# An attention and feed-forward block in fp32: one sum of the query rotation, two NF4 steps and four weight splits moved at the start of the attention loop

## The chip, the cores and the metric

The kernel runs on one core of a Trainium2 chip. The metric is the device time of one execution in microseconds. A core has TensorE (PE in the profile, its weight loads are PEld), VectorE (DVE), ScalarE (ACT), GpSimd (POOL) and SyncE (SP), which here only issues DMAs. Each engine works through its own list of instructions in order and waits on semaphores of the others.

## The reference

x has 8 sequences of 128 tokens with 512 features; ctx_4096 is the context of the same shape. Two blocks follow each other:

```
x = x + attention(layernorm(x), ctx_4096, ctx_4096, mask, Wq, Wk, Wv, Wo)
x = x + ffn(layernorm(x), w1, w2, w3)
```

The attention has 32 query heads and 8 key/value heads of 128 features, so four query heads share one key head. Queries and keys are rotated (RoPE), the logits are capped by 30 tanh(logits / 30), masked, put through a softmax, multiplied with the values and projected by Wo:

```
q = apply_rope((query @ Wq).reshape(b, t, h, d))
logits = MAX_ATTN_VAL * jnp.tanh(logits * ATTN_MULT / MAX_ATTN_VAL)
attn = einsum(softmax(where(mask, logits, -1e30)), v) @ Wo
```

The ffn first quantises its three weights (1376 x 512 or 512 x 1376) to the 16 levels of NF4, in blocks of 64 with a scale each, and turns them back to floats; then h = silu(x @ w1.T) * (x @ w2.T), and the output is h @ w3.T. All is fp32.

## The kernel before, in words

**Arithmetic.** A large product in near-fp32 is made of three fast matmuls: each operand is split into a high part (a rounded copy) and a low part (the rest), and the three products low x high, high x high and high x low are summed in PSUM (product(), L166 to L172). split() (L154) makes the two parts: a copy on ScalarE (L155) and a subtraction on an engine that the caller names, DVE or POOL (L156). One product of 512 columns over 512 contracted features is twelve matmuls.

**Stages.** The program has four stages: (1) keys, values, the layer norm of x and the first query tiles, up to 118 us; (2) the attention loop of 64 steps, from 118 to about 600 us; (3) gate and up products of the feed-forward, to 723.8 us; (4) the down product and the stores, to the end.

**The attention loop** (L762). A unit u is one key/value head and one half of the batch (four sequences); step i treats unit i // 4, sequence i % 4. The loop is a software pipeline. In step i, the order of emission is: one query tile of the next unit (q_proj, L474: twelve matmuls into one of the two banks of tag "q", then rope()); project(i - 3), the product with Wo (twelve matmuls); turn(i - 2), four transposes into a bank of tag "q" and their split; values(i - 1), the product of weights and values (matmuls into the bank "pv", on DVE a reciprocal L693 and a normalisation L694); scores(i), the logits (L678), tanh and exp on ScalarE (L681, L682), and the mask on POOL (L684). Steps 0 to 2 are special: unit 1 has its query tiles 0 and 1 in step 0, tile 2 in step 1 and tile 3 in step 2, and step 3 has none.

**rope()** (L455) rotates a query tile: two half copies on ScalarE (L463, L464), the cosine product on DVE (L465), the sine product on POOL (L466), and a closing sum (L467). For unit 1 the cosine product is written in place into the PSUM bank, and the sum runs on DVE; so the bank of tag "q" is free only when that sum is done. rope() returns the sum as a function, and the loop calls it later, through the list `later`.

**Weights.** load_o() (L657) issues the DMA of one 128 x 512 tile of Wo into a staging buffer and puts its split into `todo`; load_q() does the same for Wq. `due` (L755) says at the end of which step a split is emitted.

**NF4.** quantize() (L376) is a generator that walks over 17 pieces of the ffn weights (11 Up, 6 Down). Each piece has 15 steps, one per decision bound: an activation on ScalarE (L196) and an accumulation on DVE (L200, L202), of 128 x 1024 elements; the last piece has 96 x 512. A product with the block scales on DVE ends a piece (L280 or L238). Along the way the pieces after it are loaded (SP's DMAs) and normalised (POOL, L206). pump(n) (L405) draws steps from the generator until n credits are used up; a 128 x 1024 step costs one credit and a 96 x 512 step a half. store() (L411) emits the splits of a finished piece, one per call, and hands on what is fresh for the next call. pump() is called with 1 at the ends of steps 0 and 1, with 1.5 and 1.65 in steps 3 to 57, with 1 and 2 in step 58, with 3.45 or 2.6 for each gate/up product, and with 2 for each of the first twelve entries of the down list:

```
        if (b, i) in most:
            if i == 1:
                product(pd[b], mine, stop=False)
                mine.clear()
            pump(2)
            store()
```

The down stage takes w3 in eleven tiles w3t_0 to w3t_10. The first twelve entries use w3t_0 to w3t_7, those behind them w3t_8 to w3t_10. split_h() (L841) splits one part of h per entry, on ScalarE and DVE, four entries ahead.

Of the kernel before, what the change touches and what calls it, by code (L numbers as in the profile page):

```python
# [23 lines left out]
G = NH // NKV  # L24
# [38 lines left out]
def block_kernel(ctx: ExitStack, tc: tile.TileContext, x, ctxt, mask, wq, wk, wv, wo, w1, w2, w3, w12t, w3_t,  # L63
                 rope_tab, nf_bias, out):
    nc = tc.nc
    V, S, Q, E = nc.vector, nc.scalar, nc.gpsimd, nc.tensor
# [9 lines left out]
    def bank(tag, name):  # L76
        shape = [P, 1024 if tag == "pv" else 512]
        return ps.tile(shape, F32, tag=tag, name=name, bufs=2 if tag == "q" else 1)[:, :512]
# [75 lines left out]
    def split(hi, lo, src, engine):  # L154
        S.copy(hi, src)  # L155
        engine.tensor_tensor(lo, src, hi, ALU.subtract)  # L156
# [54 lines left out]
    class Down(Unit):  # L211
# [30 lines left out]
        def store(self, h):  # L242
            pool, tag, bufs = (f1, "w3t", 8) if h < 8 else (nf, "nf_t", 2) if h < 10 else (xp, "wide", 2)
            t = w3t[h] = pool.tile([P, 2, KT, P], F32R, tag=tag, name=f"w3t_{h}", bufs=bufs)
            own = t.rearrange("p i k c -> p i (k c)")[:self.p].rearrange("p i (c e) -> p i e c", e=4)
            split(own[:, 0], own[:, 1], self.part(self.w, h).rearrange("p (e c) -> p e c", e=4), Q)
# [44 lines left out]
    class Scales:  # L291
# [23 lines left out]
        def turn(self, tag):  # L315
            pt = bank(tag, f"pt_ar_{self.h}")[:2 * 16, :P]
            E.transpose(pt, self.s.rearrange("p t b -> p (t b)"), ident)

            def later():
                t = nf.tile([2 * 16, P], F32, tag="nf_st", name=f"art_{self.h}", bufs=1)  # L320
                S.copy(t, pt)
                nc.sync.dma_start(scale_d.rearrange("t j b h -> (t j b) h")[:, self.h * P:(self.h + 1) * P], t)
            stored.append(later)
# [81 lines left out]
    def pump(n):  # L405

        credit[0] += n
        while credit[0] > 0:
            credit[0] -= next(stream, n + credit[0])
# [7 lines left out]
    def end_store():  # L417
        if stored:
            stored.pop()()
# [7 lines left out]
    with ExitStack() as c1:  # L427
# [11 lines left out]
        def stage(src, shape, name):  # L439
            if early:  # L440
                raw = early.pop(0)
            else:
                raw = raw_pool[-1].tile([P, 512], F32, tag="raw", name=f"raw_{name}", bufs=3 if len(raw_pool) > 1 else 4)
            if len(shape) == 3:
                raw = raw.rearrange("p (k n) -> p k n", k=shape[1])
            nc.sync.dma_start(raw, src)
            return raw
# [21 lines left out]
        wqt, todo = {}, {}  # L469

        def load_q(kv, g):
            wqt[kv, g], todo["q", kv, g] = columns(wq, kv * G + g, f"wq_{kv}_{g}")

        def q_proj(u, g):  # L474
            kv, half = divmod(u, 2)
            if g == 0:
                qr[u] = a1.tile([P, 4, G, T], F32, tag="qr", name=f"qr_{u}", bufs=2)
            pq = bank("q", f"pq_{u}_{g}")
            w, t = wqt[kv, g], xT[half]
            product(pq, [((w[:, 0, k], w[:, 1, k]), (t[:, 0, k], t[:, 1, k])) for k in range(KT)])  # L480
            return lambda: rope(qr[u][:, :, g, :], pq, cosq, sgnq, f"q{u}_{g}", V if u < 2 else None, u == 1)
# [175 lines left out]
        def load_o(kv, g):  # L657
            h = kv * G + g
            raw = stage(wo[h * HD:(h + 1) * HD], [P, D], f"wo_{kv}_{g}")
            t = wot[kv, g] = at.tile([P, 2, D], F32R, tag="wo", name=f"wo_{kv}_{g}", bufs=8)  # L660
            todo["o", kv, g] = lambda: split(t[:, 0], t[:, 1], raw, Q if kv else V)

        def load_kv(kv):
            for half in range(2):
                krt[kv, half] = at.tile([P, 512], F32, tag="kr", name=f"krt_{kv}_{half}", bufs=4)
                nc.sync.dma_start(krt[kv, half], kr_d[kv, half])
            vt[kv] = at.tile([P, B, HD + 1], F32, tag="v", name=f"vt_{kv}")
            nc.sync.dma_start(vt[kv][:, :, :HD], v_d[kv])
            Q.memset(vt[kv][:, :, HD:], 1.0)

        def where(i):
            u, bb = divmod(i, 4)
            return u, u // 2, (u % 2) * 4 + bb, bb

        def scores(i):
            u, kv, b, bb = where(i)
            pl = bank("s", f"pl_{i}")
            E.matmul(pl, krt[kv, u % 2][:, bb * T:(bb + 1) * T], qr[u][:, bb].rearrange("p g t -> p (g t)"),  # L678
                     start=True, stop=True)
            th = at.tile([P, 512], F32, tag="th", name=f"th_{i}", bufs=3)  # L680
            S.activation(th, pl, AF.Tanh, scale=ATTN_MULT / CAP)  # L681
            S.activation(th, th, AF.Exp, scale=CAP)  # L682
            em[i] = th.rearrange("p (g t) -> p g t", g=G)
            Q.tensor_tensor(em[i], em[i], mt.unsqueeze(1).to_broadcast([P, G, T]), ALU.mult)  # L684

        def values(i):
            u, kv, b, bb = where(i)
            ad[i] = at.tile([P, G, HD], F32, tag="ad", name=f"ad_{i}")
            pv = ps.tile([P, G, 256], F32, tag="pv", name=f"pv_{i}", bufs=1)
            for g in range(G):  # L690
                E.matmul(pv[:, g, :HD + 1], em[i][:, g], vt[kv][:, b], start=True, stop=True)  # L691
            rs = tp.tile([P, G], F32, tag="rs", name=f"rs_{i}")
            V.reciprocal(rs.unsqueeze(2), pv[:, :, HD:HD + 1])  # L693
            V.tensor_tensor(ad[i], pv[:, :, :HD], rs.unsqueeze(2).to_broadcast([P, G, HD]), ALU.mult)  # L694
# [5 lines left out]
        def project(i):  # L700
            u, kv, b, bb = where(i)
            po = bank("wo", f"po_{i}")
            product(po, [((aT[i][:, 0, g], aT[i][:, 1, g]), (wot[kv, g][:, 0], wot[kv, g][:, 1]))
                         for g in range(G)])
            V.tensor_tensor(acc[b], acc[b], po, ALU.add)
# [19 lines left out]
        def load_w12(h):  # L725
            w12[h] = [wp.tile([P, 2, KT, P], F32R, tag="wq", name=f"w12_{h}_{j}", bufs=6) for j in range(2)]
            for j in range(2):
                nc.gpsimd.dma_start(w12[h][j], w12t_d[h, j])
# [23 lines left out]
                V.tensor_tensor(hT[half, h // 4][:, h % 4], sg, pu, ALU.mult)  # L752
            return later

        due = {0: [("o", 0, 0), ("o", 0, 1)], 1: [("o", 0, 2), ("o", 0, 3)]}  # L755
        xn = {}

        def turned(ks, tags):
            for f in [normal2(k, xn[k], tag) for k, tag in zip(ks, tags)]:
                f()  # L760

        for i in range(N):  # L762
            u, kv, b, bb = where(i)
            s8 = i % 8
            if kv + 1 < NKV:
                if s8 == 0:
                    load_kv(kv + 1)
                if s8 < 4:
                    load_q(kv + 1, s8)
                else:  # L770
                    load_o(kv + 1, s8 - 4)
                due.setdefault(i + (2 if i < 4 else 1), []).append(("q" if s8 < 4 else "o", kv + 1, s8 % 4))
            tiles = {0: (0, 1), 1: (2,), 2: (3,), 3: ()}.get(i, (bb,)) if u + 1 < 2 * NKV else ()
            later = [q_proj(u + 1, g) for g in tiles]
            later = [f() for f in later[:1]] + later[1:]
            if i == 0:
                later.pop(0)()
            if i > 3:
                store()
                end_store()  # L780
            pump(1.5 if 2 < i < 58 else 1 if i == 58 else 0)
            if 0 <= i - 3:
                project(i - 3)
            if i in (59, 61):
                ln = LayerNorm((i - 59, i - 58), f"y{i - 59}")
            if 0 <= i - 2:
                turn(i - 2)
            if 59 <= i < 63:
                ln.sums(i - 59)
            if 0 <= i - 1:  # L790
                values(i - 1)
            scores(i)
            if i == 0:
                later = [later[0]()]
            if i == 61:
                xn.update({k: pair.rows(k, "xn") for k in (0, 1)})
            for f in later:
                f()
            pump(1.65 if 2 < i < 58 else 2 if i == 58 else 1 if i < 2 else 0)
            if i == 62:  # L800
                turned((0, 1), "qq")
            if i in (60, 62):
                ln.finish(Q)
                pair = ln
            for k in due.pop(i, ()):
                todo[k]()
            if i >= 61:
                load_w12(i - 61)
# [63 lines left out]
    for b, i in down:  # L872
# [5 lines left out]
        for h in range(4 * i, min(NHT, 4 * i + 4)):  # L878
            m = min(P, H - h * P)
            t, s = w3t[h].rearrange("p i k c -> p i (k c)"), hs[b, i]  # L880
# [7 lines left out]
        elif i == 2:  # L888
            o = f1.tile([P, D], F32, tag="o", name=f"o_{b}", bufs=4)
# [41 lines left out]
```

## Time and profile before

| | us |
|---|---|
| median of 3 runs | 789.2 |
| lowest, highest | 789.14, 790.14 |
| the profiled execution | 790.01 |
| its span, first to last instruction | 788.2 |
| PE busy | 778.0 |
| DVE busy | 627.9 |
| ACT busy | 586.4 |
| POOL busy | 466.4 |

The span is what the instructions cover; 1.8 us of the execution lie around it. Groups of instructions are named by line, engine, operation and tiles (out<-in); a bracket at a line's end tells how long the engine was idle before it and who released it. Matmuls are pipelined: the twelve of one product take about 2.72 us from the first start to the start of what follows, while each shows 0.4 us of its own. The mean granted clock of TensorE over the span is 0.998 of full speed.

### The profile page before, as it was taken

How to read it: one execution, taken by the hardware profiler on the slowest of the kernel's cores; microseconds unless marked ns; L12 is line 12 of the kernel's file. 1: busy time of each engine (PE TensorE's matmuls, PEld its weight loads, DVE VectorE, ACT ScalarE, POOL GpSimd, SP SyncE). 2: the span in 40 equal slices, each digit the busy share in tenths (PEclk: the TensorE clock that was granted, in tenths of full speed). 3: DMA queues.
4: the chain of work that ended last, by engine and by line, in shares of the span. 5: the costliest groups of instructions: out<-in, count | busy, mean ns of one | idle time of the engine just before them, and what ended most of it. 6: DMA issues, size and time to landing. Idle time of an engine off the chain costs nothing. (4 is left out here: it accounts for less than half of the span.)

```text
span 788.2 us, 11198 instructions
## 1 busy us (share of the span) xinstructions
PE 778.0 (99%) x3737; PEld 627.3 (80%) x3737; DVE 627.9 (80%) x840; ACT 586.4 (74%) x821; POOL 466.4 (59%) x411
## 2 busy tenths in 40 slices
PE   8999998999999999999999999999999999999998
PEld 6788886778777878778787877888778888888877
DVE  5767777888888887888888878879878688888981
ACT  7358667989796978879797979898732678778840
POOL 3568544688787878777797877878652223232100
PEclk9999999999999999999999999999999999999999
DMA  7966735355437344526337432414133235652011
GB/s 228 300 195 195 214 105 154 108 143 176 89 121 206 135 107 121 174 55 218 103 100 203 131 94 94 125 65 134 43 119 107 57 108 157 186 162 53 5 54 54
DMA packets 73329, 102.44 MB, mean 130 GB/s; under 512 B 7832, under 2 KB 42840, under 8 KB 73272
## 3 DMA queue, kind: packets, MB, share of 16 engines
q1 hardware_dynamic: 70104, 90.19, 38.2%
q0 software_dynamic: 3168, 11.54, 4.7%
q8 instruction: 30, 0.49, 0.3%
q14 instruction: 27, 0.22, 0.1%
HBM read 79.32 MB, written 22.38 MB: 129 GB/s over the span
## 5 line engine op out<-in xcount | busy, mean ns | idle before, releaser
L202 DVE SCALAR_TENSOR_TENSOR nc_w<-nm_w,nc_w 128x1024 f32<-128x1024 bf16 (+1 forms) x238 | 284.6, 1196 | 60.2 <-ACT nm_w L196 49.8
L196 ACT ACTIVATE nm_w<-w_w,bias 128x1024 bf16<-128x1024 f32 (+1 forms) x255 | 276.2, 1115 | 14.9 <-DVE nc_w L202 7.9
L172 PE MATMUL pq<-xT,wq 128*128 128x512 f32 x768 | 209.3, 422 | 0.0
L172 PE MATMUL po<-wo,aT 128*128 128x512 f32 x768 | 190.1, 396 | 0.0
L172 PEld LDWEIGHTS pq<-xT,wq 128*128 128x128 f32 x768 | 143.9, 188 | 55.9 <-issue 24.4
L172 PEld LDWEIGHTS po<-wo,aT 128*128 128x128 f32 x768 | 143.8, 189 | 34.5 <-issue 2.9
L684 POOL TENSOR_TENSOR th<-th,mt 128x512 f32<-128x512 f32 x64 | 83.8, 1310 | 87.9 <-ACT th L682 80.0
L466 POOL TENSOR_TENSOR rs_q<-rs_q,sgnq 128x512 f32<-128x512 f32 x64 | 82.9, 1295 | 14.7 <-ACT rs_q L464 14.7
L681 ACT ACTIVATE th<-pl 128x512 f32<-128x512 f32 x64 | 38.3, 598 | 53.5 <-PE pl L678 51.3
L467 POOL TENSOR_TENSOR qr<-rc_q,rs_q 128x512 f32<-128x512 f32 x56 | 72.5, 1295 | 0.0
L691 PE MATMUL pv<-vt,th 128*128 128x129 f32 x512 | 67.9, 276 | 0.1
L678 PE MATMUL pl<-qr,krt 128*128 128x512 f32 x128 | 66.4, 601 | 0.0
L172 PE MATMUL pg<-xT,w 128*128 128x512 f32 x264 | 63.7, 390 | 0.0
L172 PE MATMUL pu<-xT,w 128*128 128x512 f32 x264 | 63.5, 389 | 0.0
L691 PEld LDWEIGHTS pv<-vt,th 128*128 128x128 f32 x512 | 62.2, 192 | 0.7 <-POOL th L684 0.7
L172 PE MATMUL pd<-w3t,hs 128*128 128x512 f32 (+3 forms) x297 | 60.8, 366 | 0.4 <-POOL w3t L156 0.4
L172 PEld LDWEIGHTS pd<-w3t,hs 128*128 128x128 f32 (+1 forms) x297 | 51.3, 189 | 9.9 <-POOL w3t L156 0.8
L206 POOL TENSOR_TENSOR w_w<-w_w,s_w 128x1024 f32<-128x1024 f32 (+1 forms) x17 | 39.6, 2329 | 33.0 <-DMA s_w<-scale_d 31.6
L172 PEld LDWEIGHTS pu<-xT,w 128*128 128x128 f32 x264 | 49.6, 188 | 10.3
L172 PEld LDWEIGHTS pg<-xT,w 128*128 128x128 f32 x264 | 49.3, 188 | 10.1
L156 POOL TENSOR_TENSOR w3t<-w_w,w3t 128x512 fp32r<-128x512 f32 (+1 forms) x11 | 17.2, 1564 | 65.7 <-ACT w3t L155 65.7
L155 ACT CAST aT<-pt_a 128x512 fp32r<-128x512 f32 x64 | 36.6, 571 | 24.9 <-PE pt_a L162 24.9
(119 smaller groups left out, 1103.7 us busy)
## 6 DMA issues: line engine op xcount, KB each, us to landing
w12t_d<-dqt SPq DMA_DIRECT2D x22, 512.0 KB
w<-w12t_d POOLq DMA_DIRECT2D x22, 512.0 KB, 4.6
s_w<-scale_d SPq DMA_DIRECT2D x40, 256.0 KB
raw_wq<-in_L_xattn_Wq SPq DMA_DIRECT2D x32, 256.0 KB
raw_wo<-in_L_xattn_Wo SPq DMA_DIRECT2D x32, 256.0 KB
s_w<-scale_d SPq DMA_DIRECT2D x86, 64.0 KB
ws<-in_L_ffn_w SPq DMA_DIRECT2D x20, 256.0 KB
w_w<-in_w12t SPq DMA_DIRECT2D x10, 512.0 KB
```

Source lines behind the costliest of these rows:

```text
L155: S.copy(hi, src)
L156: engine.tensor_tensor(lo, src, hi, ALU.subtract)
L172: E.matmul(out, a, b, start=start and i + j == 0, stop=stop and i == n - 1 and j == 2)
L196: S.activation(m, self.w, AF.Relu, bias=bias[:self.p, i:i + 1], scale=BIG if up else -BIG)
L202: V.scalar_tensor_tensor(self.c, m, step, self.c, ALU.min, ALU.subtract if i == POS[0] else ALU.add)
L206: Q.tensor_tensor(self.w, self.w, self.s, ALU.mult)
L466: Q.tensor_tensor(s, s, every(sgn), ALU.mult)
L467: return lambda: (engine or Q).tensor_tensor(dst, c, s, ALU.add)
L678: E.matmul(pl, krt[kv, u % 2][:, bb * T:(bb + 1) * T], qr[u][:, bb].rearrange("p g t -> p (g t)"), start=True, stop=True)
L681: S.activation(th, pl, AF.Tanh, scale=ATTN_MULT / CAP)
L684: Q.tensor_tensor(em[i], em[i], mt.unsqueeze(1).to_broadcast([P, G, T]), ALU.mult)
L691: E.matmul(pv[:, g, :HD + 1], em[i][:, g], vt[kv][:, b], start=True, stop=True)
```

## The change

Four edits. The closing sum of a query tile in steps 1 and 2 (tiles 2 and 3 of unit 1) is emitted behind values(i - 1) and ahead of scores(i), instead of behind scores(i). The pumps at the ends of steps 0 and 1 are gone, so that the NF4 stream begins its work in the loop at step 3. The four splits of the first projection weights wo_0 to wo_3, which were emitted two at the end of step 0 and two at the end of step 1, all stand in step 1: two ahead of scores(1) and two at its end. And the subtractions of wo_2 and wo_3 run on POOL instead of DVE.

```
-            todo["o", kv, g] = lambda: split(t[:, 0], t[:, 1], raw, Q if kv else V)
+            todo["o", kv, g] = lambda: split(t[:, 0], t[:, 1], raw, Q if kv or g > 1 else V)
...
-        due = {0: [("o", 0, 0), ("o", 0, 1)], 1: [("o", 0, 2), ("o", 0, 3)]}
+        due = {1: [("o", 0, g) for g in range(G)]}
...
             if 0 <= i - 1:
                 values(i - 1)
+            if i in (1, 2):
+
+                later.pop(0)()
+                if i == 1:
+                    for _ in range(2):
+                        todo[due[1].pop(0)]()
             scores(i)
...
             for f in later:
                 f()
-            pump(1.65 if 2 < i < 58 else 2 if i == 58 else 1 if i < 2 else 0)
+            pump(1.65 if 2 < i < 58 else 2 if i == 58 else 0)
```

## The prediction

> **What bounds the kernel now.** First the page's busy shares, then the stage table, then the timelines of the two places where TensorE stops.
>
> ```profile
> PE 778.0 (99%) x3737; PEld 627.3 (80%) x3737; DVE 627.9 (80%) x840; ACT 586.4 (74%) x821; POOL 466.4 (59%) x411
> ```
>
> ```profile
> 118.00:136.10 18.10, 15.62 (x64) 10.49 (x63) 13.55 (x19) 14.22 (x22) 9.14 (x7) 0.91 0.56 169
> ...
> 200.00:300.00 100.00, 100.00 (x499) 80.09 (x497) 84.12 (x112) 83.70 (x119) 78.05 (x65) 1.00 0.43 123
> ...
> 723.80:758.40 34.60, 34.22 (x152) 28.01 (x150) 31.64 (x39) 27.86 (x40) 5.96 (x4) 1.00 0.06 14
> 758.40:788.00 29.60, 26.63 (x147) 23.14 (x147) 10.24 (x18) 2.59 (x5) 0.00 (x0) 1.00 0.19 71
> ```
>
> Columns are PE, PEld, DVE, ACT, POOL busy, granted clock, DMA share, GB/s. PE is full from 200 to 300 us with a fifth of the other engines free: there only PE's own work counts. The first row, attention steps 0 to 2, is the weak one (15.62 of 18.10 us, clock 0.91). In the third DVE works 31.64 of 34.60 us: it is full there. PE's timeline in the weak place:
>
> ```profile
> 123.91 3.00 PE L172 MATMUL pq<-xT,wq 128*128 128x512 f32 x12
> 129.36 0.63 PE L162 MATMUL pt_a<-ident,ad 128*128 128x128 f32 x4 [2.44 <-DVE qr L467]
> ...
> 131.60 4.69 PE L172 MATMUL po<-wo,aT 128*128 128x512 f32 x12
> 136.13 0.60 PE L162 MATMUL pt_a<-ident,ad 128*128 128x128 f32 x4
> ```
>
> The first attention transposes wait 2.44 us for a bank that DVE frees with the sum of the third query tile. DVE's timeline shows why that sum is late:
>
> ```profile
> 123.68 1.22 DVE L202 SCALAR_TENSOR_TENSOR nc_w<-nm_w,nc_w 128x1024 f32<-128x1024 bf16 x1
> 124.81 2.39 DVE L156 TENSOR_TENSOR wo<-raw_wo,wo 128x512 fp32r<-128x512 f32 x2
> 127.12 0.69 DVE L465 TENSOR_TENSOR pq<-pq,cosq 128x512 f32<-128x512 f32 x1
> ...
> 128.53 0.68 DVE L467 TENSOR_TENSOR qr<-pq,rs_q 128x512 f32<-128x512 f32 x1
> ```
>
> One NF4 step and two weight subtractions lie ahead of it. After the gap the granted clock is halved:
>
> ```profile
> 131.00:132.00 1.00, 1.00 (x3) 0.35 (x2) 1.00 (x2) 0.00 (x0) 0.00 (x0) 0.50 0.35 77
> ...
> 133.00:134.00 1.00, 1.00 (x4) 0.56 (x3) 0.97 (x3) 0.97 (x3) 0.04 (x1) 0.50 0.91 330
> ```
>
> With 0.87 before and 0.92 behind these rows, it is at half for some 3.4 us. The second place is the end of the NF4 stream (timelines of DVE and PE):
>
> ```profile
> 724.09 0.69 DVE L752 TENSOR_TENSOR hT<-sg,pu 128x512 f32<-128x512 f32 x1 [0.35 <-PE pu L172]
> ...
> 754.38 0.55 DVE L156 TENSOR_TENSOR hs<-hT,hs 128x384 fp32r<-128x384 f32 x1
> 754.85 0.68 DVE L238 TENSOR_TENSOR w_w<-nc_w,s_w 96x512 f32<-96x512 f32 x1
> ```
>
> ```profile
> 758.35 26.67 PE L172 MATMUL pd<-w3t,hs 96*128 96x512 f32 x147 [0.38 <-POOL w3t L156]
> ```
>
> At 724.09 DVE waits for PE, so it starts the last stage in step with it. From there it never pauses until the last NF4 product (L238) at 755.53; ScalarE's copy and POOL's subtraction bring the last weight tile w3t_10 at 758.30, and PE has already waited 0.38 us for it. The stream has no slack there.
>
> **Part 1, the sum between values and scores (steps 1 and 2).** scores() puts nothing on DVE, so DVE's order stays: multiply, reciprocal, normalise, sum. Nothing else passes it on another engine. Price 0.
>
> **Part 2, the start.** Off DVE ahead of the third tile go one NF4 step (1.22) and two subtractions (2.39), and from behind it another NF4 step; wo_0 and wo_1 now follow the sum, and wo_2 and wo_3 are POOL's, between the masks of steps 1 and 2. On ScalarE two NF4 activations (1.15, 1.13) go, and the copies of wo_0 and wo_1 (1.12) now stand after the third tile's half copies and ahead of step 1's tanh. SP moves one pair of scale loads behind three query-weight loads; it waits there for staging buffers, freed by 130 us, and the scales are used only at the unit's end, after 140 us. The chain from the old rows, as an estimate:
> - ScalarE: third tile's half copies end 123.2 (PE's sums end 121.89), wo_0 and wo_1 copies 124.3, tanh and exp 125.6, wo_2 and wo_3 copies 126.7, the fourth tile's half copies 128.2, aT copy 128.8.
> - DVE: multiply 124.4, normalise 125.2, sum 125.9; then the two wo subtractions to 127.8, multiply 128.9, aT subtraction 129.5.
> - POOL, 1.29 each: mask 1 to 126.9, wo_2 128.2, wo_3 129.5, fourth tile's sine 130.8, mask 2 132.1.
> - PE: fourth query tile unchanged at 123.91, its twelve matmuls at the pitch of 0.227 end 126.65. The bank is free since 125.9: transposes 126.65, values 127.1, scores 128.0, projection from 128.8, held by aT until 129.6, next transposes 132.0 instead of 136.13.
>
> The gain is 4.1 us. Ends: only the idle gap, 2.4; no bubble at all, 4.95 (126.65 plus 0.43, 0.90, 0.46 and 2.74 from the rows of the next step gives 131.2). I stay near the upper end because the halved clock goes with the gap. What is late next is aT, then mask 2 on POOL, with 0.3 us to spare against the values at 132.35.
>
> **Part 3, the two NF4 steps come back.** The stream is one fixed list, advanced by credits. Two credits fewer at steps 0 and 1 leave it two items behind everywhere until the last stage, whose twelve pumps of 2 had room to spare. In attention and gate/up nothing is paid: each pump issues as many items as before, PE is full there, and the moved scale and weight loads stay a whole unit ahead of use. POOL's normalise (2.40) of the second down unit now stands behind two more w12 loads that wait for PE until 631.8; it ends near 634.8, about when ScalarE first needs it. w3t_7 moves into the last stage, ready near 727.1 against its use at 728.6.
>
> In the last stage two 128x1024 steps more lie ahead of the last product. The pitch of such pairs is 2.46 (728.36 to 730.82). Since store() runs once per iteration, w3t_10 also slips one iteration, past one more hs subtraction (0.47, from 750.92 to 751.39). That is 2.93. POOL's w3t_7 and the last normalise now fall into DVE's full stretch; a subtraction beside POOL took 1.63 instead of 0.69 at 746.39. Bounds 2.4 (the steps alone) to 3.9 (one such clash); I take 3.2, nearer to the counted items. PE's wait becomes some 3.5 us instead of 0.38.
>
> Then the clock. A 2.44 us gap was followed by 3.4 us at half clock, at most 1.7 us of dense matmuls. The new gap is longer, but part of the slow time may fall into the gap itself. Bounds 0 and 1.7; I take 1.1.
>
> The Trainium skill, "TensorE: Matmul & The Clock Gate", section "Why this matters for your kernels", speaks against this change: it asks for no PE gaps over about 3 us, since an idle window returns the clock to half. By it the old gap would have been safe and the new one would not: the full 1.7 at the end and a sum of 790.8 instead of 790.2. The rows above show the drop already behind 2.44 us, and the measurement decides.
>
> **Sum.** The profiled execution took 790.01 (span 788.2 and 1.8 around it): 790.01 - 4.1 + 3.2 + 1.1 = 790.2. It stands 0.8 above the median of 789.2. If the runs at the median lack the early half clock, their gain is 3.3 and they end at the same 789.2 - 3.3 + 3.2 + 1.1 = 790.2; if they also escape the late one, at 789.1. I say 789.8, nearer to the first.
>
> **Rivals.**
> - A, above: gain at the start, given back at the end. 789.8, own range 788.6 to 791.0. Chance 0.52.
> - B, faster: the end stays covered, because DVE makes up the two steps. For it: DVE is idle for 12% of 662 to 723.8 us (54.43 busy of 61.80). Against: it waits for PE at 724.09 with the stream still two items behind. 790.01 - 4.1 = 785.9; decides if w3t_10 slips less than about 1.5 us. Chance 0.15.
> - C, slower: POOL becomes the bound at the start. If its five operations take 1.71 (mask 1 at 126.61, beside DVE's wo subtractions) instead of 1.29, mask 2 ends 2.1 later and values 2 wait 1.8: 790.2 + 1.8 = 792.0. It decides from about 0.9 us of waiting. Against: only some 2 us of DVE's subtractions overlap. Chance 0.20.
> - D, no half clock at either end in most runs: 789.2 - 3.3 + 3.2 = 789.1. Chance 0.13.
>
> The Trainium skill, "GPSIMD Engine Reference", section "Specifications", says that POOL shares its SBUF ports with VectorE when that reads two SBUF inputs. By it every subtraction of wo beside POOL is slow, which gives C; the old rows give both 1.29 and 1.71.
>
> **How the numbers follow.** 0.2% is 1.58 us, about what a measurement of this kernel can tell. A lies within it but for 0.06 above and 0.02 below; D all but 0.02 below; B is faster but for 0.02, C slower but for 0.01. Faster 0.17, same 0.58, slower 0.25. The range takes in most of B and C: 786.6 to 792.0.
>
> **What would show it.** Right: the transposes behind the fourth query tile start without a gap, the clock stays at 1.00 near 130 us, and the next come some 4 us earlier; at the end the 96-row matmul waits 3 to 4 us for POOL's w3t, with clock rows of 0.50 behind. Wrong: that wait stays under 1 us, PE waits for mask 2 near 132 us, or new PE waits appear between 140 and 720 us.

## The result, and the profile after

The changed kernel takes 794.6 us (median of six runs, 793.38 to 798.08) where the kernel before, run beside it, takes 789.55 (789.14 to 790.14). The ratio is 1.0069, 95% interval 1.0050 to 1.0088: it is slower. The prediction said 789.8 us within 786.6 to 792.0, so the measurement lies outside its range.

The profiled execution is the lowest of the six, 793.38 us with a span of 791.3. PE's timeline at the start, with start, duration, engine, line, operation and tiles, and in brackets the idle time ahead and who ended it:

```profile
126.72 0.60 PE L162 MATMUL pt_a<-ident,ad 128*128 128x128 f32 x4
...
130.25 2.56 PE L172 MATMUL po<-wo,aT 128*128 128x512 f32 x10 [0.71 <-DVE aT L156]
132.66 0.60 PE L162 MATMUL pt_a<-ident,ad 128*128 128x128 f32 x4
```

The gap of 2.44 us ahead of the first transposes is gone, and the next ones come at 132.66 instead of 136.13: the start gains 3.4 us. DVE's timeline shows what is late next:

```profile
125.06 0.68 DVE L467 TENSOR_TENSOR qr<-pq,rs_q 128x512 f32<-128x512 f32 x1
125.65 3.35 DVE L156 TENSOR_TENSOR wo<-raw_wo,wo 128x512 fp32r<-128x512 f32 x2
128.92 0.68 DVE L465 TENSOR_TENSOR pq<-pq,cosq 128x512 f32<-128x512 f32 x1
129.52 0.68 DVE L156 TENSOR_TENSOR aT<-pt_a,aT 128x512 fp32r<-128x512 f32 x1
```

The two wo subtractions take 3.35 us. POOL is busy beside them: with the mask of step 1 (L684) from 125.47 to 126.77, then with its own two.

```profile
126.74 3.40 POOL L156 TENSOR_TENSOR wo<-raw_wo,wo 128x512 fp32r<-128x512 f32 x2
```

That holds the fourth tile's multiply to 128.92 and aT to 129.52 (its duration brings it to 130.2, where the projection starts).

Then the surprise, in the attention loop. POOL's timeline and PE's at step 52:

```profile
508.44 2.41 POOL L206 TENSOR_TENSOR w_w<-w_w,s_w 128x1024 f32<-128x1024 f32 x1 [4.33 <-DMA s_w<-scale_d]
510.82 1.26 POOL L684 TENSOR_TENSOR th<-th,mt 128x512 f32<-128x512 f32 x1
```

```profile
512.13 1.16 PE L691 MATMUL pv<-vt,th 128*128 128x129 f32 x8 [0.91 <-POOL th L684]
```

Before, POOL began this L206 at 504.53 without a wait, and the mask followed in time:

```profile
504.53 2.41 POOL L206 TENSOR_TENSOR w_w<-w_w,s_w 128x1024 f32<-128x1024 f32 x1
...
509.68 1.30 POOL L684 TENSOR_TENSOR th<-th,mt 128x512 f32<-128x512 f32 x1 [0.27 <-DVE ad L694]
```

Now L206 waits 4.33 us for the scales of the eleventh and last Up piece, and the mask of step 51, queued behind it on POOL, makes the values in step 52 wait on PE. SP's issues around that place, before and after, tell why the scales are late:

```profile
497.60 0.93 SPq L275 DMA_DIRECT2D w_w<-in_w12t  x2
498.59 2.56 SPq L265 DMA_DIRECT2D s_w<-scale_d  x4
...
501.90 6.85 SPq L361 DMA_DIRECT2D scale_d<-art  x8
```

```profile
495.22 6.89 SPq L361 DMA_DIRECT2D scale_d<-art  x8
502.23 0.97 SPq L275 DMA_DIRECT2D w_w<-in_w12t  x2
503.25 2.61 SPq L265 DMA_DIRECT2D s_w<-scale_d  x4
```

The eight scale stores (L361) are emitted by the loop's end_store(), in the same step before and after; the loads (L275, L265) come from the NF4 stream. With the stream two items late the loads fall behind the stores, and the stores wait 4.2 us for ScalarE's copy (L355), as the waits of SP's queue in the profile after show:

```profile
SPq L361 <- ACT art L355: 4.2, 1, 4.2
```

The end, PE's timeline:

```profile
722.27 34.16 PE L172 MATMUL pd<-w3t,hs 128*128 128x512 f32 x150
759.69 28.43 PE L172 MATMUL pd<-w3t,hs 96*128 96x512 f32 x147 [3.26 <-POOL w3t L156]
```

The wait for the last weight tile is 3.26 us instead of 0.38, and the 147 matmuls behind it take 28.43 instead of 26.67. The stage table (columns PE, PEld, DVE, ACT, POOL busy, granted clock, DMA share, GB/s) has the reason:

```profile
760.00:761.00 1.00, 1.00 (x5) 0.78 (x4) 0.34 (x2) 0.30 (x1) 0.00 (x0) 0.79 0.00 0
761.00:762.00 1.00, 1.00 (x4) 0.81 (x3) 1.00 (x3) 0.74 (x2) 0.00 (x0) 0.50 0.00 0
762.00:763.00 1.00, 1.00 (x3) 0.72 (x3) 0.46 (x1) 0.00 (x0) 0.00 (x0) 0.50 0.69 260
763.00:764.00 1.00, 1.00 (x4) 0.81 (x3) 0.00 (x0) 0.00 (x0) 0.00 (x0) 0.51 0.01 2
764.00:765.00 1.00, 1.00 (x6) 0.82 (x5) 0.65 (x2) 0.66 (x2) 0.00 (x0) 1.00 0.00 0
```

Half clock from 760.6 to 764.0, 3.4 us.

This execution is a lucky one. A second profile of the same kernel (a2_after below) took 794.37 us, near the median, and the account is made with it beside the first. Each row is a difference of two places in PE's timeline against the same places before (first scores 118.12, next transposes 136.13, and the down product as below):

```profile
723.82 34.16 PE L172 MATMUL pd<-w3t,hs 128*128 128x512 f32 x150
```

| | predicted | first profile, 793.38 | a2_after, 794.37 |
|---|---|---|---|
| stage 1, to the first scores (L678) | 0 | -0.04 | -0.72 |
| first scores to the next transposes | -4.1 | -3.43 | -3.44 |
| from there to the down product | 0 | +1.92 | +2.44 |
| wait for the last w3t | +3.2 | +2.88 | +3.91 |
| the 147 matmuls, slower by the clock | +1.1 | +1.76 | +2.17 |
| sum | +0.2 | +3.1 | +4.4 |

The sums answer to the spans (791.3 and 792.6 against 788.2). Stage 1 differs by up to 1.0 us between executions of kernels that are alike there, so it is left out of the comparisons of the start below.

### The profile page after: what moved, and what is told of

Read it like the earlier page. It is cut to its first block, busy times and chain, and to the rows that moved or that the text cites. A ratio compares the mean times of both kernels' runs of the same rounds, so it can differ in the third digit from the quotient of the medians.

```text
span 791.3 us, 11202 instructions
## 1 busy us (share of the span) xinstructions
PE 779.4 (98%) x3737; PEld 628.3 (79%) x3737; DVE 624.7 (79%) x838; ACT 586.1 (74%) x821; POOL 470.0 (59%) x413
## 5 line engine op out<-in xcount | busy, mean ns | idle before, releaser
L684 POOL TENSOR_TENSOR th<-th,mt 128x512 f32<-128x512 f32 x64 | 83.5, 1305 | 82.6 <-ACT th L682 70.3
L172 PE MATMUL pd<-w3t,hs 128*128 128x512 f32 (+3 forms) x297 | 62.6, 373 | 3.3 <-POOL w3t L156 3.3
L678 PE MATMUL pl<-qr,krt 128*128 128x512 f32 x128 | 65.7, 595 | 0.1
L206 POOL TENSOR_TENSOR w_w<-w_w,s_w 128x1024 f32<-128x1024 f32 (+1 forms) x17 | 40.1, 2361 | 36.8 <-DMA s_w<-scale_d 34.6
```

What stands on the lines that cost most here:

```text
L172: E.matmul(out, a, b, start=start and i + j == 0, stop=stop and i == n - 1 and j == 2)
L206: Q.tensor_tensor(self.w, self.w, self.s, ALU.mult)
```

## The experiments

The theory after this reading: the start's gain is real; the two items that the stream owes cost some 2 us in the loop and 5 to 6 us at the end, and none of that has to do with the sum or the weights. The first four kernels take the change apart.

**e1_repaid: the stream's debt is paid at once.** The changed kernel, with half a credit more in steps 4 to 7.

```
-            pump(1.65 if 2 < i < 58 else 2 if i == 58 else 0)
+            pump(2.15 if 3 < i < 8 else 1.65 if 2 < i < 58 else 2 if i == 58 else 0)
```

> The changed kernel, with the two NF4 steps repaid in steps 4 to 7 (half a credit more at each of their last pumps), so that the stream is where it was before from step 8 on. Theory (the start gains about 3.5 us, and all that is lost comes from the stream being two steps late): the gain stays, the wait of TensorE near 512 us and the long wait for the last w3t are gone, and the time is 786.0 (785.3 to 787.0) against 789.5 before. Rival (the start's gain is lost again in any case, at the next place where the pipeline is tight): 789 to 790.

Measured: 786.65 us (785.83 to 787.12), ratio 0.9962 [0.9948, 0.9976]. The start keeps its gain (first scores to next transposes 14.58 us, as after; before 18.01), nothing is lost in the loop, and the end is that of before:

```profile
754.18 26.66 PE L172 MATMUL pd<-w3t,hs 96*128 96x512 f32 x147 [0.38 <-POOL w3t L156]
```

So all of the loss is the debt's. This version beats both kernels: it is 3.1 us faster than the one before.

**e2_stream: the debt alone.** The kernel before, without its pumps in steps 0 and 1.

```
-            pump(1.65 if 2 < i < 58 else 2 if i == 58 else 1 if i < 2 else 0)
+            pump(1.65 if 2 < i < 58 else 2 if i == 58 else 0)
```

> The kernel before, with only the two pumps at the ends of steps 0 and 1 taken away; the sum, the weight splits and their engines stay. Theory: it gains about 1.2 us at the start (one NF4 step of 1.22 us off DVE ahead of the third tile's multiply, the two subtractions of 2.39 us stay) and pays all of the late stream: 1.9 us in the attention loop, 2.9 at the last w3t and up to 1.8 of half clock, so 793 to 796. Rival (the loss comes from the weight splits on POOL, not from the stream): 788 to 789.5.

Measured: 796.31 us (795.68 to 796.84), ratio 1.0084 [1.0070, 1.0097]. The debt alone makes the kernel slower, as expected, by a little more than the 793 to 796 us allowed, and the sizes inside differ: the start gained 2.1 us rather than 1.2, the loop lost 1.5, and the end lost more.

```profile
761.33 29.33 PE L172 MATMUL pd<-w3t,hs 96*128 96x512 f32 x147 [4.30 <-POOL w3t L156]
```

The clock stays at half for 6.8 us here, from 760.2 to 767.0, twice as long as in the first profile after.

**e3_weights: the sum and the weight splits alone.** The changed kernel, with the two pumps put back (the reverse of e2's edit).

> The changed kernel with the two pumps at the ends of steps 0 and 1 put back: only the sum and the weight splits are moved. Theory: the third tile's sum is one NF4 step (1.2 us) later than in the changed kernel, so that 2.3 to 3.0 us of the start's gain are left, and nothing is lost later: 786.5 to 787.5. Rival (the splits on POOL cost the time): 791 or more.

Measured: 788.76 us (787.83 to 789.95), ratio 0.9989 [0.9980, 0.9998]. It gains 1.0 us and misses the expected 786.5 to 787.5. DVE's and PE's timelines:

```profile
129.74 1.22 DVE L202 SCALAR_TENSOR_TENSOR nc_w<-nm_w,nc_w 128x1024 f32<-128x1024 bf16 x1
130.87 0.69 DVE L465 TENSOR_TENSOR pq<-pq,cosq 128x512 f32<-128x512 f32 x1
131.47 0.68 DVE L156 TENSOR_TENSOR aT<-pt_a,aT 128x512 fp32r<-128x512 f32 x1
```

```profile
132.20 2.57 PE L172 MATMUL po<-wo,aT 128*128 128x512 f32 x10 [1.31 <-DVE aT L156]
134.61 0.60 PE L162 MATMUL pt_a<-ident,ad 128*128 128x128 f32 x4
```

The second NF4 step stands on DVE ahead of the fourth tile's multiply and of aT, and PE pays for it. Measured from the first scores, the start gains 1.41 us here and 2.08 in e2; together 3.49, against 3.43 for both edits at once. The two parts simply add, and more than half of the gain comes with the NF4 steps: the same edit that makes the debt.

**e4_lategate: the debt from the gate/up stage on.** The kernel before, two credits short in gate/up, so that the attention loop is untouched and the end has the same order of work as the changed kernel.

```
-        pump((3.45 if n < last - 3 else 2.6) if n > 0 else 0)
+        pump((1.45 if n == 1 else 3.45 if n < last - 3 else 2.6) if n > 0 else 0)
```

> The kernel before, with two credits taken from the pump of the second of the gate/up products in the loop behind the attention, so that the stream is two steps late from there on and nowhere earlier. Theory: the wait for the last w3t grows from 0.4 to about 3.3 us as in the changed kernel, and the half clock behind it adds 0 to 1.8: 792.4 to 794.3. Rival (the late w3t is hidden, and the loss of the changed kernel lies in the attention loop): 789 to 790.

Measured: 795.89 us (794.78 to 796.41), ratio 1.0076 [1.0064, 1.0089], above what was expected. The end's price is larger than the first profile had told:

```profile
761.55 28.26 PE L172 MATMUL pd<-w3t,hs 96*128 96x512 f32 x147 [4.24 <-POOL w3t L156]
```

Two timelines show a microsecond that the first profile after did not pay, POOL's and then DVE's:

```profile
729.97 1.29 POOL L206 TENSOR_TENSOR w_w<-w_w,s_w 96x512 f32<-96x512 f32 x1 [3.50 <-DMA s_w<-scale_d]
```

```profile
730.15 1.66 DVE L156 TENSOR_TENSOR hs<-hT,hs 128x512 fp32r<-128x512 f32 x1
```

POOL's normalise of the last piece falls on a DVE subtraction and stretches it from 0.69 to 1.66. DVE has no pause from there to the last product, so the wait grows by as much.

**e5_repaygate: the debt in attention alone.** The changed kernel, with the two credits paid in gate/up.

```
-        pump((3.45 if n < last - 3 else 2.6) if n > 0 else 0)
+        pump((3.95 if n < 5 else 3.45 if n < last - 3 else 2.6) if n > 0 else 0)
```

> The changed kernel, with the two NF4 steps repaid only behind the attention (half a credit more at each of the second to fifth gate/up products of the loop), so that the stream is late through the whole attention loop and in time for the last stage. Theory: the start's gain of 3.5 us stays, 1.4 to 2.0 us are lost in the attention loop (most of it near 512 us), the last wait is 0.4 us again: 787.3 to 788.5. Rival (the last stage is the whole loss, and the attention loop's was chance): 786.0 to 786.8.

Measured: 789.09 us (788.69 to 792.36), ratio 1.0001 [0.9992, 1.0009]. It lies 0.6 us above the expected range and well above the rival's 786.0 to 786.8, in which the debt in attention costs nothing. The end is clean again, and PE's waits between 140 and 600 us hold the 0.9 us of step 52:

```profile
756.50 26.88 PE L172 MATMUL pd<-w3t,hs 96*128 96x512 f32 x147 [0.41 <-POOL w3t L156]
```

```profile
PE pv L691 <- POOL th L684: 0.9, 1, 0.9
```

Against e1, the debt in attention costs 2.4 us by the medians. In the two profiles 1.6 us of that lie in the loop (719.64 - 131.82 in e1, 721.92 - 132.49 here); 0.65 is a longer stage 1, which the edit doesn't touch. By the medians e1, this and e4 put the change together again: a gain of 3.1 (e1), a loss of 2.4 in attention, a loss of 6.1 from gate/up on (e4); +5.4 where the whole change measures +5.1.

**e6_load: the late load alone put right.** The changed kernel, with the loads of the last Up piece issued two stream items earlier (k = 8 instead of 10), ahead of the scale stores.

```
-                    if k == (6 if isinstance(units[i + 1], Down) else 10):
+                    if k == (6 if isinstance(units[i + 1], Down) else 8 if i == 9 else 10):
```

> The changed kernel, with the load of the eleventh NF4 piece issued two steps earlier in the stream, so that SP issues it ahead of the eight scale stores that wait for ScalarE, as in the kernel before. Theory: POOL's normalise of that piece no longer waits 4.3 us for its scales, the mask behind it is in time, TensorE does not wait near 512 us, and 1.4 us of the loss go: 793.2 (792.4 to 794.0), the last wait unchanged. Rival (the mask is late for another reason): TensorE still waits there, 794 to 795.

Measured: 792.94 us (792.58 to 794.21), ratio 1.0046 [1.0034, 1.0058]: 1.7 us better than the changed kernel. On SP the scales are issued at 495.40, ahead of the stores at 498.71, and POOL's L206 has no wait any more:

```profile
503.90 2.38 POOL L206 TENSOR_TENSOR w_w<-w_w,s_w 128x1024 f32<-128x1024 f32 x1
...
506.48 1.31 POOL L684 TENSOR_TENSOR th<-th,mt 128x512 f32<-128x512 f32 x1 [0.19 <-ACT th L682]
```

The rest of the debt is as it was, and the end still waits 4.37 us. From the next transposes to the down product PE needs 587.80 us, against 587.69 before and 589.61 after:

```profile
132.86 0.60 PE L162 MATMUL pt_a<-ident,ad 128*128 128x128 f32 x4
...
720.66 34.16 PE L172 MATMUL pd<-w3t,hs 128*128 128x512 f32 x150
```

So the chain at step 52 (stores, loads, normalise, mask, values) is shown as the cause of the loop's loss. Two smaller losses of the changed kernel, 0.4 us near 375 us in its first profile and some 0.7 us near 370 and 430 us in a2_after, are missing here and in e2, which both owe the same two items there; so they vary from execution to execution and are no steady price of the debt.

**e7_allvector: all four wo subtractions on DVE.** This goes back to the start. It is e1 with POOL's two subtractions returned to DVE; the rival held that POOL delays the start, which was rival C of the prediction in a milder form.

```
-            todo["o", kv, g] = lambda: split(t[:, 0], t[:, 1], raw, Q if kv or g > 1 else V)
+            todo["o", kv, g] = lambda: split(t[:, 0], t[:, 1], raw, Q if kv else V)
```

> The repaid kernel (two NF4 steps repaid in steps 4 to 7) with all four first weight subtractions on DVE as in the kernel before. Theory: POOL's two cost nothing by themselves, but two on POOL beside two on DVE slow each other (3.35 and 3.40 us for two instead of 1.84 and 2.58); four on DVE alone take 3.7 us, so the fourth tile's multiply and the first aT come 0.3 to 0.5 us later: 786.9 to 787.3. Rival (POOL's queue is what holds the start back): 785.5 to 786.2.

Measured: 788.21 us (787.3 to 789.26), ratio 0.9982 [0.9974, 0.9991]: 1.6 us worse than e1, where 0.3 to 0.7 worse had been expected, and the rival falls. DVE's timeline:

```profile
125.40 4.55 DVE L156 TENSOR_TENSOR wo<-raw_wo,wo 128x512 fp32r<-128x512 f32 x4
129.88 0.69 DVE L465 TENSOR_TENSOR pq<-pq,cosq 128x512 f32<-128x512 f32 x1
130.48 0.68 DVE L156 TENSOR_TENSOR aT<-pt_a,aT 128x512 fp32r<-128x512 f32 x1
```

Four on DVE take 4.55, against 3.35 for two beside POOL's two. They aren't alone either: POOL's mask (125.21 to 126.51) and the fourth tile's sine (127.90 to 129.41) fall beside them. A pair with POOL idle took 1.36 us in e9, so each POOL operation beside them cost some 0.9 to 1.0 us, as an estimate: 4.55 is 2.72 and two of them, and 3.35 is 1.36 and two of them. At this place sharing the four is still the better way.

**e8_onelate: one credit late at the end.** As e4, with 2.45 in place of 1.45, to see whether the wait grows evenly with the debt and where the clock drops.

> The kernel before, with one credit (not two) taken from the second gate/up product of the loop, so that the stream is one step late in the last stage and the store of w3t_10 stays in its iteration. Theory: the last wait grows by one step of 1.23 us, to 1.6, or to 2.6 if the last piece's normalise on POOL falls on one of DVE's hs subtractions; the clock stays whole behind a wait under 2 us: 790.9 to 792.1. Rival (any wait there halves the clock): 792.5 to 793.5.

Measured: 793.71 us (791.73 to 794.30), ratio 1.0047 [1.0035, 1.0059], above the theory's 790.9 to 792.1 and a little above the rival's 792.5 to 793.5. Half the debt costs two thirds of the price:

```profile
759.85 28.26 PE L172 MATMUL pd<-w3t,hs 96*128 96x512 f32 x147 [2.63 <-POOL w3t L156]
```

```profile
745.38 1.64 DVE L156 TENSOR_TENSOR hs<-hT,hs 128x512 fp32r<-128x512 f32 x1
...
749.92 1.50 DVE L156 TENSOR_TENSOR hs<-hT,hs 128x384 fp32r<-128x384 f32 x1
```

Of the wait's 2.63 us, 0.38 was there before, 1.23 is the NF4 step itself, and the remaining 1.0 is a clash: two DVE subtractions now fall on POOL's w3t work, where before there was one. Behind 2.63 us the clock still drops. In one of the five runs it did not (mean clock 1.0, so it had none at the start either), and that run took 791.73 against 793.09 to 794.30 for the others, at 0.996. Only the profiled run, 793.09, shows where its half clock lies: 3.4 us at the start and 3.4 at the end.

**e9_early: the start without its new late piece.** e1, with wo_0 and wo_1 split in step 0 ahead of the scores, wo_2 and wo_3 at the end of step 1, all on DVE.

```
-            todo["o", kv, g] = lambda: split(t[:, 0], t[:, 1], raw, Q if kv or g > 1 else V)
+            todo["o", kv, g] = lambda: split(t[:, 0], t[:, 1], raw, Q if kv else V)
...
-        due = {1: [("o", 0, g) for g in range(G)]}
+        due = {0: [("o", 0, 0), ("o", 0, 1)], 1: [("o", 0, 2), ("o", 0, 3)]}
...
-                if i == 1:
-                    for _ in range(2):
-                        todo[due[1].pop(0)]()
+            if i == 0:
+                for k in due.pop(0):
+                    todo[k]()
             scores(i)
```

> The repaid kernel with all four first weight splits on ScalarE and DVE as in the kernel before, but wo_0 and wo_1 emitted in step 0 ahead of scores, where both engines stood idle (ScalarE 2.6 us before step 0's tanh, DVE 3.0 us before the second tile's multiply), and wo_2 and wo_3 at the end of step 1. Theory: no subtraction of a weight stands beside one on POOL, DVE has the two of step 1 done in 1.84 us instead of 3.35, and the first aT comes earlier by 0.3 to 0.8 us: 786.0 (785.4 to 786.5). Rival (the copies hold back step 0's tanh, and what is gained is lost there): 786.7 to 787.5.

Measured: 786.46 us (786.01 to 786.79), ratio 0.9961 [0.9947, 0.9974]. It is in the expected range, but nothing tells it apart from e1. aT is now on time, and something else is late: ScalarE waits for the weights themselves.

```profile
118.31 1.29 ACT L155 CAST wo<-raw_wo 128x512 fp32r<-128x512 f32 x2 [2.18 <-DMA raw_wo<-in_L_xattn_Wo]
```

The first mask is then late by 0.67 us for the values, and first scores to next transposes is 14.52 us instead of 14.58.

**a2_after: the changed kernel once more**, to learn which of the two end prices is the usual one.

> The changed kernel itself once more. Theory: its first profile was the fastest of six runs, because the last piece's normalise on POOL missed DVE's hs subtractions; here it should hit one, the last wait be 4.2 to 4.4 us instead of 3.26, the wait near 512 us 0.9 us again, and the median 794.0 to 795.0. Rival: the wait is 3.3 us again and the spread comes from the clock alone.

Measured: 794.62 us (793.97 to 795.26), ratio 1.0064 [1.0051, 1.0076]. PE at step 52 and at the end:

```profile
512.02 1.16 PE L691 MATMUL pv<-vt,th 128*128 128x129 f32 x8 [1.17 <-POOL th L684]
...
760.55 28.84 PE L172 MATMUL pd<-w3t,hs 96*128 96x512 f32 x147 [4.29 <-POOL w3t L156]
```

So the usual wait is that of e2 and e4 (4.2 to 4.3), and the first profile's 3.26 the exception: there POOL's normalise began at 729.32, 0.04 us behind the DVE subtraction, and was itself the slow one (1.80 instead of 1.29, with 0.69 on DVE).

## Why the prediction was wrong

Against the predicted sum of 790.2 the run a2_after took 4.2 us more. By the table above: 2.44 from the loop, 1.1 from the clock, 0.7 from the last wait, 0.7 from the start, less the 0.7 by which stage 1 was shorter.

- **Part 1, the moved sum: no run contradicts it.** Price 0 was said, and the order on DVE (multiply, reciprocal, normalise, sum) is the one that the profile shows. No experiment moved the sum alone.
- **Part 2, the start: right in mechanism, 0.7 too large.** The bubble went, the clock is 1.00 near 130 us, aT is late next and mask 2 arrives in time, as said. Mis-sized was "then the two wo subtractions to 127.8": that is 1.9 us, and they took 3.35, with POOL's mask and then POOL's own two beside them. The old profile held the warning (1.63 for a subtraction beside POOL, used for the last stage), and the sum for the start didn't use it. The sum also stayed near its upper end "because the halved clock goes with the gap"; that part is small: e4 has the old gap of 2.44 us without half clock (below), and needs 17.66 us from the first scores to the next transposes instead of 18.01.
- **Part 3, the loop: this step failed.** It said: "In attention and gate/up nothing is paid: each pump issues as many items as before, PE is full there, and the moved scale and weight loads stay a whole unit ahead of use." They do not. In quantize() an Up piece's successor is loaded at k = 10 and normalised at k = 13, three items later, of which the debt takes none; but the loads share SP's queue with the scale stores of the loop, which do not move with the stream. Two items were enough to put the loads behind stores that wait 4.2 us. Loss: 1.9 and 2.4 us in the two profiles of the changed kernel, of which 1.5 and 1.8 come at step 52; e6 takes away 1.7 by moving only these loads, and leaves the loop within 0.1 us of that before. New PE waits between 140 and 720 us were one of the prediction's own signs of being wrong. For gate/up the sentence holds: e4 lost nothing ahead of the down product.
- **Part 3, the last wait: right in mechanism, low by 0.7.** 3.2 was added; 2.9 and 3.9 were measured. The two steps cost what was said. The clash beside POOL, which set the upper bound of 3.9, is the usual case (four of the five profiles that owe both steps at the end) and not the exception.
- **Part 3, the clock: bound too low.** "A 2.44 us gap was followed by 3.4 us at half clock, at most 1.7 us of dense matmuls" was read from one gap. The 147 matmuls lost 1.76 in the first profile, 2.17 in a2_after and 2.66 in e2, since the half clock can last 6.8 us. The upper bound of 1.7 should have been some 2.7.
- **The rivals.** B (the end stays covered) fell: the debt came through the loop to the last stage undiminished. C (POOL bounds the start, slower) gave the right side for the wrong reason: mask 2 was in time, and e7 shows that taking POOL's part away makes it worse. D fell with the clock's drop at the end in both profiles of the changed kernel. A is what happened, plus a loss in the loop that no rival held.

The Trainium skill's "TensorE: Matmul & The Clock Gate", section "Why this matters for your kernels", was weighed in the prediction with its rule of no PE gaps over about 3 us. The runs agree that the longer gap is dear and disagree on the limit: behind the 2.63 us of e8 the profile shows the clock at 0.50, and three more of its five runs have the same mean clock of 0.996, so a gap below 3 us is not safe here.

The Trainium skill's "GPSIMD Engine Reference", section "Specifications", says that POOL's SBUF interfaces are shared with VectorE and contended by VectorE instructions with two SBUF inputs. The start agrees: pairs of wo subtractions took 3.35 on DVE and 3.40 on POOL, overlapping, while a pair on DVE with POOL idle took 1.36 in e9.

## What to carry to other kernels

Work that is taken out of a bad moment has to be paid back soon after, while the engines still have room: half a credit more in four steps turned a loss of 5.1 us into a gain of 3.1. When a stream of work is shifted against a loop, compare the order of the DMA issues on each queue, not only the distance between a load and its use: here eight stores that waited 4.2 us held up the loads behind them. And where the end of a kernel has no slack, a late last operand can cost more than its wait: here waits of 2.6 to 4.4 us were followed by 1.6 to 2.7 us lost to half clock.

## What was not expected of the hardware

The half clock comes in lengths of about 3.4 us: at the end of the kernel one in the first profile after and in e4, e6 and e8, two (6.8 us) in e2 and a2_after. In a2_after it begins inside PE's wait and goes on behind it. The stage table of a2_after:

```profile
758.00:759.00 1.00, 0.00 (x0) 0.00 (x0) 0.23 (x1) 1.00 (x2) 0.03 (x1) 0.72 0.02 8
759.00:760.00 1.00, 0.00 (x0) 0.00 (x0) 0.75 (x1) 1.00 (x3) 1.00 (x1) 0.50 0.00 0
...
764.00:765.00 1.00, 1.00 (x4) 0.71 (x4) 0.00 (x0) 0.00 (x0) 0.00 (x0) 0.50 0.50 188
765.00:766.00 1.00, 1.00 (x5) 0.87 (x4) 0.21 (x1) 0.21 (x1) 0.00 (x0) 0.86 0.00 0
```

The drop at 758.4 comes 2.1 us into a wait that began at 756.3 (722.10 plus 34.16 for the matmuls ahead of it), while PE stood still; PE works from 760.55 and has the full clock back at 765.3. What decides between one length and two was not settled: waits of 4.24 (e4, one) and 4.29 (a2_after, two) lie side by side, and runs of one kernel differ (mean clocks of 0.994, 0.996 and 0.998 in e4, start and end together). Nor does a gap of one length always halve the clock. The 2.44 us at the start did so before and in e8; e4, the same kernel up to there, shows the gap and then the full clock, where the same row was at 0.50 before:

```profile
128.97 0.63 PE L162 MATMUL pt_a<-ident,ad 128*128 128x128 f32 x4 [2.44 <-DVE qr L467]
```

```profile
131.00:132.00 1.00, 0.81 (x3) 0.19 (x1) 1.00 (x3) 0.60 (x1) 0.00 (x0) 1.00 0.09 25
```

An interval that runs on its own and that the wait meets at one place or another would fit all of this, but nothing here shows it.
